# Expert arms of a perceiver's mixtures in three column tiles of 32, 32 and 64, with the small pairs' arm in front, and two weights asked for behind a context

## The chip, the cores and the metric

The kernel runs on one core of a Trainium2 chip. The metric is the device time of one execution in microseconds, the median of several runs. Beside it there is one profiled execution, whose trace holds every instruction of the engines: PE (TensorE's matmuls), PEld (TensorE's weight loads), DVE (VectorE), ACT (ScalarE), POOL (GpSimd), and SP, whose queue asks for nearly all transfers.

## What is computed

The reference is a perceiver of four levels over 2 x 64 tokens of 256 features, all in float32, with a context of 2 x 1024 rows of 192 features. Each level adds a cross attention, a second mixing layer and a feed-forward layer to `x`. The 128 tokens fill the 128 partitions. The feed-forward layers of levels 1, 2 and 3 are mixtures of 8 experts, of which each token uses its best 2:

```python
logits = xf @ gate_w
top_w, top_idx = jax.lax.top_k(logits, 2)
h = jax.nn.gelu(einsum('td,edf->tef', xf, w1) + b1)      # level 1, hidden width 1024
y = einsum('tef,efd->ted', h, w2) + b2
out = einsum('ted,te->td', y, combine)
```

Level 2 has a hidden width of 512 with a gate (`silu(g) * u`) and no biases; level 3 has a width of 1024 with a gate and biases. How many tokens an expert gets is known only when the kernel runs.

## The kernel before, in words

**Slots.** `experts` handles the 8 experts as four pairs, expert r with expert r + 4. A pair has 128 slots (columns of the gathered tokens `xg`), and a slot belongs to one of the two experts. `split[r]`, read into a register of TensorE's sequencer, says how the slots are shared: 1 means 64 and 64 ("equal"); 0 means `least` for the first expert and the rest for the second ("unequal": 32 and 96 where `least` is 32, levels 1 and 2; 0 and 128 in level 3); 2, in the levels with biases (1 and 3) and not for pair 0, means that both experts have at most 32 tokens ("small pairs").

**Tiles.** `Level.tiles_of` turns that into column tiles of the stationary operand: an equal pair gives two tiles of 64, an unequal pair of levels 1 and 2 four tiles of 32 (one for the first expert, three for the second), one of level 3 a single tile of 128. `hidden` runs, for each column half (`part`, 512 moving columns) and each of the two chunks of features, one matmul for each tile; `out_of` runs for each block of hidden features (8 in level 1, 4 in level 2) one matmul with 256 moving columns for each tile. A small pair goes through `hidden_by_halves` and `out_of_halves` instead, where each expert's 32 slots take two tiles of 32, one for each half of the hidden width. Each float32 matmul of the program shows as two MATMUL and two LDWEIGHTS rows in the trace.

**Arms.** `by_tiles` writes the arms of the branch. TensorE's sequencer compares `split[r]` and runs one arm; the others lie between in the code and are jumped over. The order of the arms in the code is: equal; unequal; small pairs. An `if` inside the `else` of the first one tells the last two apart, and where there is no arm for small pairs (a second column half), that inner `if` has no `else`.

**Order of work.** For pair r TensorE runs the hidden arm of r, gathers the tokens of r + 1, runs the output arm of r - 1, turns the products of r, and opens the sums of r + 1. After pair 3's hidden arm comes a test for tokens that found no slot, the last output arm, and the scatter. Inside the arms and between them `in_written_order` fixes the order of each engine's instructions; the SP queue is not part of that, its order is left to the scheduler.

**Weights.** `shelf.load` asks for the experts' weights in pieces of 1 MB; they lie in rotating buffers, so a transfer starts when an earlier user of its buffer is done. `l2x_w` asks for the four weights of level 2's cross attention (L132) after level 1's experts' weights. The context `crows` (`l2x_ctx`, L1976) of that attention lies in a stage pool of its own and is asked for at the beginning of that stage. Its first reader is `weigh` (L2065); `wv` is read in `project` (L2097) and `wo` in `output` (L2107).

The lines that matter below: L716 (`hidden`), L697 (`hidden_by_halves`), L690 (its biases), L773 (`out_of`), L706 (`out_of_halves`), L726 (biases), L747 (gather), L759 (turn), L787 (scatter), L409 and L411 (values of a later attention that fill a gap), L319 (matmuls that only keep TensorE busy), L800 and L808 (the comparisons).

Of the kernel before, what the change touches and what calls it, by code (L numbers as in the profile page):

```python
# [18 lines left out]
P = 128  # L19
# [39 lines left out]
def tile_perceiver(ctx: ExitStack, tc: tile.TileContext, i: dict, out: bass.AP):  # L59
# [8 lines left out]
    def stage_pool(**given):  # L68

        return tc.tile_pool(reuse_waits="tile", **given)  # L70
# [5 lines left out]
    @contextmanager  # L76
    def psum(pairs, singles):
        if psum_now["split"] != (pairs, singles):
            scope = psum_now["scope"]
            scope.close()  # L80
            psum_now.update(
                split=(pairs, singles),
                a=scope.enter_context(stage_pool(name="ps_a", bufs=pairs, space=PSUM)),
                b=scope.enter_context(stage_pool(name="ps_b", bufs=singles, space=PSUM)),
            )
        yield
# [7 lines left out]
    def stat(n=1, name="stat"):  # L94
        return small.tile([P, n], F32, tag=f"s{n}", bufs=12 if n == 1 else 4, name=name)
# [29 lines left out]
    def weight(name, index=None):  # L125
        src = i[name] if index is None else i[name][index]
        size = 4
        for n in src.shape[1:]:
            size *= n
        tag = "w2" if size <= 2048 else "w4" if size <= 4096 else "w8"  # L130
        t = wpool.tile(list(src.shape), F32, tag=tag, bufs=W_BUFS[tag], name=f"{name}_sb")
        nc.sync.dma_start(t, src)  # L132
        return t
# [148 lines left out]
    @contextmanager  # L282
    def in_written_order(behind=None):


        traced = nc.cur_bb.bb.instructions
        first = len(traced)
        last = {}
        for ins in reversed(traced):
            if ins.engine == ET.PE:  # L290
                last[ET.PE] = ins
                break
        yield last

        def put_behind(ins, other):
            tc.add_manual_dep(
                ins, other.name,
                mybir.DependencyInfo(
                    mybir.DependencyClass.NoSync, mybir.DependencyReason.DATA
                ),  # L300
                reason="in_written_order",
            )

        for ins in nc.cur_bb.bb.instructions[first:]:
            if ins.engine in (ET.PE, ET.DVE, ET.Activation, ET.Pool):
                if ins.engine in last:
                    put_behind(ins, last[ins.engine])
                elif behind and ins.engine == ET.PE:
                    for other in behind.values():
                        if other.engine != ET.Pool:  # L310
                            put_behind(ins, other)
                last[ins.engine] = ins
# [320 lines left out]
    def quarter_tile(j):  # L633
        return slice(j * 32, j * 32 + 32), j
# [4 lines left out]
    class Level:  # L639
# [24 lines left out]
        def tiles_of(self, equal):  # L664

            if equal:
                return [(slice(j * 64, j * 64 + 64), j) for j in range(2)]
            if self.least == 0:
                return [(slice(0, P), 1)]
            return [(quarter_tile(j)[0], min(j, 1)) for j in range(4)]  # L670

    def experts(level, x, shelf, pool, over_pool, fill):
        count, width, name = consts.count, level.width, level.name
# [6 lines left out]
        xg, hT, y, own, prods, split = {}, {}, {}, {}, {}, {}  # L680
# [117 lines left out]
        def by_tiles(r, behind, work, by_halves=None):  # L798

            with tc.If(split[r] == 1) as shared:  # L800
                with in_written_order(behind):
                    work(level.tiles_of(True))
            with shared.Else():
                if r == 0 or not level.halved:
                    with in_written_order(behind):
                        work(level.tiles_of(False))
                    return
                with tc.If(split[r] == 0) as other:  # L808
                    with in_written_order(behind):
                        work(level.tiles_of(False))  # L810
                if by_halves is not None:
                    with other.Else():
                        with in_written_order(behind):
                            by_halves()

        with in_written_order() as done:
            ps = bank()
# [235 lines left out]
        for h, half in enumerate(sums):  # L1053
            by_tiles(0, seen, lambda tiles: hidden(0, half, tiles))
            with in_written_order() as seen:
                if level.biases is not None:
                    add_biases(0, [half])
                gates(0, half, h)
                if half is sums[-1]:
                    ways_back()  # L1060
                    gather(1)
                    for k in range(turns):
                        if k == turns - 1:
                            fill(3)
                        turn(0, k)
                    sums = open_sums(1)
        for r in range(1, PAIRS):
            for h, half in enumerate(sums):
                by_tiles(
                    r, seen, lambda tiles: hidden(r, half, tiles),  # L1070
                    None if h else lambda: hidden_by_halves(r, half if level.gated else half[:1]),
                )
                with in_written_order() as seen:
                    gates(r, half, h)
                    if r == 1 and h == 0:
                        start_sum()
                    if h == len(sums) - 1:
                        if r + 1 < PAIRS:
                            gather(r + 1)
                        po = bank()  # L1080
            by_tiles(
                r - 1, seen, lambda tiles: out_of(r - 1, po, tiles),
                lambda: out_of_halves(r - 1, po),
# [50 lines left out]
    with psum(2, 4), stage_pool(name="l0x", bufs=1) as pool, stage_pool(  # L1134
# [5 lines left out]
        wv = pool.tile([CH + 1, 2, D], F32, name="l0x_wv")  # L1140
        m8 = pool.tile([P, NB, NK], U8, name="m8")
        wk = weight("l0x_wk")
        wlkv = weight("l0x_wlkv")
        wq = weight("l0x_wq")
# [10 lines left out]
        wo = weight("l0x_wo")  # L1155
# [349 lines left out]
    with psum(2, 4), stage_pool(name="l0a", bufs=1) as pool, in_written_order():  # L1505
        wq, wkv, wo = weight("l0a_wq"), weight("l0a_wkv"), weight("l0a_wo")
# [102 lines left out]
        r = stat(name="rstd")  # L1609
# [243 lines left out]
    with psum(3, 2), stage_pool(name="l1x", bufs=1) as pool, stage_pool(  # L1853
        name="l1x_att", bufs=3
    ) as att:
        wq, wo = weight("l1x_wq"), weight("l1x_wo")
# [90 lines left out]
    nc.sync.dma_start(l1f_bs, i["l1f_bs"])  # L1947
    for r in range(1, PAIRS):
        shelf.load(r)
    l2x_w = [weight(f"l2x_w{n}") for n in "qkvo"]  # L1950
    with psum(2, 4), stage_pool(name="l1f", bufs=1) as pool:
        last = kv3.values(1, 2)

# [16 lines left out]
    with psum(2, 4), stage_pool(name="l2x", bufs=1) as pool, stage_pool(  # L1970
        name="l2x_att", bufs=2
    ) as att, in_written_order():
        wq, wk, wv, wo = l2x_w

        crows = pool.tile([P, 16, CD + 1], F32, name="l2x_ctx")
        nc.sync.dma_start(crows[:, :, :CD], i["ctx"])  # L1976
        nc.gpsimd.memset(crows[:, :, CD:], 1.0)
        qT = pool.tile([P, 8, P], F32, name="l2x_qT")

# [578 lines left out]
    with psum(3, 2), stage_pool(name="l3x", bufs=1) as pool, stage_pool(  # L2558
        name="l3x_att", bufs=3
    ) as att:  # L2560
        wq, w1, w2, wz, wh = l3x_w
# [37 lines left out]
    with psum(2, 4), stage_pool(name="l3a", bufs=1) as pool:  # L2599
        with in_written_order():  # L2600
# [29 lines left out]
            for c in range(2):  # L2630
                for b in range(NB):
                    r = slice(b * S, (b + 1) * S)
# [188 lines left out]
```

## Time and profile before

| | before |
|---|---|
| median of 3 runs | 657.37 us (655.67 to 657.70) |
| the profiled execution, whole | 657.39 us |
| its span, first to last instruction | 655.4 us |
| mean granted TensorE clock | 0.996 |
| PE busy | 616.8 us, 94% of the span, 4722 matmul rows |
| DVE, ACT, POOL busy | 308.5, 254.8 and 49.6 us |
| HBM read | 85.98 MB, 131 GB/s over the span |

A line of the timeline gives start and duration in microseconds from the span's start, then engine, line of the kernel, operation, out<-in, the shape (rows*columns of the array for TensorE, then the moving operand) and the count; in brackets how long the engine had been idle before it and what ended that. "issue" is idle time in which the engine waited for nothing that the profile shows. A line of the groups by form gives the busy time in us and the mean of one instruction in ns behind the first bar, and the idle time ahead of the group behind the second. A matmul's duration is its latency; neighbours overlap, so the pace is read from their starts.

### The profile page before, as it was taken

The page shows a single profiled execution, that of the slowest core. Times are in us where ns is not written, and L with a number is a line of the kernel's source. Part 1 is how long each engine was busy: PE and PEld are TensorE (multiplying, and loading weights), DVE is VectorE, ACT ScalarE, POOL GpSimd, SP SyncE. Part 2 cuts the span into 40 slices and gives each one's busy share as a digit, 9 for nine tenths or more (in the row PEclk, how much of TensorE's full clock was granted, in tenths as well). Part 3 has the DMA queues.
Part 4 walks back from the last instruction along what each step waited for, and adds up shares of the span by engine and source line. Part 5 has one row for each costly group of instructions (what it writes and reads, how often), then busy time and mean ns, then how long its engine had stood idle before and what let it go on. Part 6 is the DMA issues. An engine that isn't in the chain of part 4 may idle for free. (4 is left out here: it accounts for less than half of the span.)

```text
span 655.4 us, 11703 instructions
## 1 busy us (share of the span) xinstructions
PE 616.8 (94%) x4722; PEld 451.1 (69%) x4722; DVE 308.5 (47%) x864; ACT 254.8 (39%) x503; POOL 49.6 (8%) x77
## 2 busy tenths in 40 slices
PE   7989999999999879999999988999989999999996
PEld 3547659766754448999998677999974456774444
DVE  5875452268671014555554435535435247747111
ACT  2464362378722222323223424413422149742111
POOL 3450000000100000000000040040000000000000
PEclk9999999999999989999999999999999999999999
DMA  8960025920438367000000500012047920093870
GB/s 287 407 284 1 17 74 166 316 95 2 171 117 340 111 215 283 1 1 2 1 1 1 192 1 1 1 36 94 1 136 291 384 91 1 2 380 144 349 300 11
DMA packets 19441, 87.05 MB, mean 133 GB/s; under 512 B 2080, under 2 KB 6704, under 8 KB 11088
## 3 DMA queue, kind: packets, MB, share of 16 engines
q1 hardware_dynamic: 19120, 86.09, 35.1%
q8 instruction: 49, 0.80, 0.5%
q14 instruction: 16, 0.13, 0.1%
q10 hardware_dynamic: 256, 0.03, 0.0%
HBM read 85.98 MB, written 0.13 MB: 131 GB/s over the span
## 5 line engine op out<-in xcount | busy, mean ns | idle before, releaser
L2065 PE MATMUL bank<-l2x_ctx,p 128*128 128x193 f32 x256 | 48.1, 327 | 0.0
L2065 PEld LDWEIGHTS bank<-l2x_ctx,p 128*128 128x128 f32 x256 | 40.8, 190 | 0.4
L1701 DVE CUSTOM_DVE_ANT_0 p<-two_banks,zero 128x1024 f32<-128x1024 f32 x32 | 38.6, 1217 | 5.2 <-PE two_banks L1691 5.0
L1709 ACT ACTIVATE p<-p,negmax 128x1024 f32<-128x1024 f32 x32 | 36.9, 1153 | 4.7 <-DVE negmax L1701 4.7
L2029 DVE TENSOR_REDUCE l2x_mx<-two_banks 128x128 f32<-128x1024 f32 x16 | 19.6, 1224 | 26.2 <-PE two_banks L2021 26.2
L2014 PE MATMUL two_banks<-l2x_qA,ctxA 128*128 128x128 f32 x256 | 31.9, 278 | 0.0
L2014 PEld LDWEIGHTS two_banks<-l2x_qA,ctxA 128*128 128x128 f32 x256 | 30.3, 192 | 1.1 <-issue 1.0
L765 DVE COPY m_hT<-bank 128x512 f32<-128x512 f32 x12 | 8.3, 691 | 44.7 <-PE bank L759 35.5
L319 PE MATMUL bank<-ctxA,ones 128*128 128x256 f32 x94 | 26.2, 395 | 1.0 <-DVE x_new L279 1.0
L2051 DVE TENSOR_TENSOR p<-two_banks,l2x_shift 128x512 f32<-128x512 f32 x32 | 20.6, 686 | 13.4 <-ACT l2x_shift L2046 13.4
L223 ACT ACT_TABLE_LOAD x20 | 25.7, 1283 | 0.4
L739 ACT ACTIVATE m_g<-two_banks 128x512 f32<-128x512 f32 x12 | 7.2, 597 | 47.8 <-PE two_banks L716 32.0
L740 DVE TENSOR_TENSOR m_prod<-two_banks,m_g 128x512 f32<-128x512 f32 x12 | 8.3, 690 | 35.5 <-ACT m_g L739 35.5
L2058 ACT ACTIVATE p<-p 128x512 f32<-128x512 f32 x32 | 19.6, 630 | 12.2 <-DVE p L2051 12.2
L1716 PEld LDWEIGHTS two_banks<-ident,p 128*128 128x128 f32 x128 | 13.7, 141 | 11.0 <-ACT pT L1745 9.1
L780 ACT COPY m_y<-bank 128x256 f32<-128x256 f32 x12 | 4.5, 372 | 41.6 <-PE bank L773 36.8
L319 PEld LDWEIGHTS bank<-ctxA,ones 128*128 128x128 f32 x94 | 16.1, 193 | 5.3 <-issue 2.6
L1691 PE MATMUL two_banks<-n_kT,n_qx 32*128 32x512 f32 x128 | 19.1, 640 | 0.0
L1716 PE MATMUL bank<-ident,p 128*128 128x128 f32 x128 | 18.5, 280 | 0.5
L2021 PE MATMUL two_banks<-l2x_qB,ctxB 64*128 64x128 f32 x256 | 18.6, 285 | 0.0
L1304 POOL TENSOR_SCALAR xh<-xh,cx_mv,rstd 128x192 f32<-128x192 f32 x16 | 16.8, 1062 | 15.7 <-DVE rstd L231 15.7
L2085 ACT COPY l2x_uT<-bank 96x256 f32<-96x256 f32 x16 | 5.9, 369 | 30.5 <-PE bank L2082 30.5
(608 smaller groups left out, 1336.5 us busy)
## 6 DMA issues: line engine op xcount, KB each, us to landing
l1f_w_sb<-in_l1f_w_dram SPq DMA_DIRECT2D x12, 1024.0 KB, 5.4
l3f_w_sb<-in_l3f_w_dram SPq DMA_DIRECT2D x12, 1024.0 KB, 9.3
more_w<-in_l3f_w_dram SPq DMA_DIRECT2D x12, 1024.0 KB, 9.3
l0f_w_sb<-in_l0f_w_dram SPq DMA_DIRECT2D x8, 1024.0 KB, 8.4
l2f_w_sb<-in_l2f_w_dram SPq DMA_DIRECT2D x8, 1024.0 KB, 4.8
more_w<-in_l1f_w_dram SPq DMA_DIRECT2D x4, 1024.0 KB, 6.0
more_w<-in_l2f_w_dram SPq DMA_DIRECT2D x6, 512.0 KB, 8.3
xh<-in_ctx_dram SPq DMA_DIRECT2D x8, 192.0 KB, 5.6
```

Of the source, the lines that this page charges most:

```text
L223: nc.scalar.activation(junk, behind, func, scale=0.0)
L319: nc.tensor.matmul(ps[:, :D], ones, ctxA[:, 0, 0, :D], start=True, stop=True)
L1691: nc.tensor.matmul(sc[u][:, n * 512 : (n + 1) * 512], qx[c, n][rows_, b].rearrange("p h q -> p (h q)"), kT[c, b][rows_, n, :], start=True, ...
L1701: nc.vector.tensor_tensor_reduce(p[u], sc[u], zero.to_broadcast([P, NK]), -1.0, 3.0e38, ALU.add, ALU.min, least)
L1709: nc.scalar.activation(p[u], p[u], AF.Exp, bias=sc[u], scale=-1.0, accum_out=total[u // 4][:, u % 4 : u % 4 + 1],)
L1716: nc.tensor.transpose(ps[:, kc * P : (kc + 1) * P], p[u][:, (4 * k + kc) * P : (4 * k + kc + 1) * P], ident,)
L2014: nc.tensor.matmul(sc[k][:, n, t, :], ctxA[:, b, n, t * P : (t + 1) * P], qA[:, j, b].rearrange("p h q -> p (h q)"), start=(t == 0), stop= ...
L2021: nc.tensor.matmul(sc[k][:, n, t, :], ctxB[half[n], b, t * P : (t + 1) * P], qB[half[n], j, b].rearrange("p h q -> p (h q)"), start=False, ...
L2029: nc.vector.tensor_reduce(mx[k], sc[k].rearrange("p n t q -> p q (n t)"), AX.X, ALU.max)
L2051: nc.vector.tensor_tensor(p[k][:, n], sc[k][:, n], shifts[k].unsqueeze(1).to_broadcast([P, 4, P]), ALU.add,)
L2058: nc.scalar.activation(p[k][:, n], p[k][:, n], AF.Exp)
L2065: nc.tensor.matmul(po[k][:, : CD + 1], p[k][:, kc // 4, kc % 4, :], crows[:, b * 8 + kc, :], start=(kc == 0), stop=(kc == 7),)
```

## The change

It has two parts.

1. An unequal pair of levels 1 and 2 gets three column tiles: 32 for the first expert, then 32 and 64 for the second. In `by_tiles` the inner branch of levels 1 and 3 compares with 2 instead of 0, and the small pairs' arm stands ahead of the unequal one in the code. Where there is no arm for small pairs, the inner `if` stays as it was.
2. `l2x_w` asks for `wq` and `wk` alone; `wv` and `wo` are asked for in the next stage, in the line behind the context's transfer.

```diff
-            return [(quarter_tile(j)[0], min(j, 1)) for j in range(4)]
+            return [(slice(0, 32), 0), (slice(32, 64), 1), (slice(64, P), 1)]
...
-                with tc.If(split[r] == 0) as other:
+                if by_halves is None:
+                    with tc.If(split[r] == 0):
+                        with in_written_order(behind):
+                            work(level.tiles_of(False))
+                    return
+                with tc.If(split[r] == 2) as other:
+                    with in_written_order(behind):
+                        by_halves()
+                with other.Else():
                     with in_written_order(behind):
                         work(level.tiles_of(False))
-                if by_halves is not None:
-                    with other.Else():
-                        with in_written_order(behind):
-                            by_halves()
...
-    l2x_w = [weight(f"l2x_w{n}") for n in "qkvo"]
+    l2x_w = [weight(f"l2x_w{n}") for n in "qk"]
...
-        wq, wk, wv, wo = l2x_w
+        wq, wk = l2x_w
 
         crows = pool.tile([P, 16, CD + 1], F32, name="l2x_ctx")
         nc.sync.dma_start(crows[:, :, :CD], i["ctx"])
+        wv, wo = weight("l2x_wv"), weight("l2x_wo")
         nc.gpsimd.memset(crows[:, :, CD:], 1.0)
```

In the built program TensorE loses 80 float32 matmuls of code, 56 matmul rows of them on the path that this data takes (4722 to 4666). The lists of the other engines and of the SP queue keep their instructions and their order.

## The prediction

> **What bounds the kernel now.** I read the page first, then the groups by form, then TensorE's waits, then the timeline of level 1's experts, with its weight loads. The page says which engine has no slack:
>
> ```profile
> PE 616.8 (94%) x4722; PEld 451.1 (69%) x4722; DVE 308.5 (47%) x864; ACT 254.8 (39%) x503; POOL 49.6 (8%) x77
> ...
> q8 instruction: 49, 0.80, 0.5%
> ```
>
> PE is busy 94% of the span. In the experts its rows follow each other almost without idle time (48.1 of 55.0 us in 190 to 245, 33.4 of 35.0 us in 495 to 530), so a microsecond put into an expert arm on PE is a microsecond of the kernel; nothing hides it. The second line is used further down. The groups by form give what an arm costs in each shape:
>
> ```profile
> L716 PE MATMUL two_banks<-l2f_w_sb,m_xg 128*64 128x512 f32 x32 | 7.3, 598 | 0.5 <-ACT m_xg L752 0.5
> L716 PE MATMUL two_banks<-l2f_w_sb,m_xg 128*32 128x512 f32 x64 | 7.3, 595 | 0.2 <-PE bank L759 0.2
> ```
>
> 64 rows of 32 columns take as long as 32 rows of 64: four 32-column tiles run side by side, as two of 64 do. The timeline (start, duration) gives the pace, the order of arms and the pauses:
>
> ```profile
> 199.43 1.05 PE L690 MATMUL two_banks<-l1f_bs,own 8*32 8x512 f32 x4
> 200.41 1.92 PE L697 MATMUL two_banks<-l1f_w_sb,m_xg 128*32 128x512 f32 x16
> ...
> 214.07 0.63 PE L706 MATMUL bank<-more_w,m_hT 128*32 128x256 f32 x4
> 216.28 1.92 PE L706 MATMUL bank<-more_w,m_hT 128*32 128x256 f32 x28 [1.58 <-issue]
> ...
> 220.84 3.64 PE L716 MATMUL two_banks<-l1f_w_sb,m_xg 128*32 128x512 f32 x32
> 224.41 3.67 PE L773 MATMUL bank<-l1f_w_sb,m_hT 128*64 128x256 f32 x32
> ...
> 230.20 1.03 PE L409 MATMUL two_banks<-l3x_wv_sb,ctxA 128*128 128x256 f32 x4
> 231.16 0.70 PE L411 MATMUL two_banks<-l3x_wv_sb,ctxB 64*128 64x256 f32 x4
> 231.79 2.56 PE L773 MATMUL bank<-l1f_w_sb,m_hT 128*32 128x256 f32 x41
> 236.83 2.62 PE L773 MATMUL bank<-l1f_w_sb,m_hT 128*32 128x256 f32 x23 [2.48 <-issue]
> ```
>
> The 32-column rows of L716 and L773 say which arms run unequal: in level 1 pair 3 (hidden at 220.84, output at 231.79), in level 2 pairs 1 and 2 (hidden at 502.46 and 509.74, output at 513.96 and 520.62). Pair 1 of level 1 runs by halves (L697, L706). Level 3 has no 32-column tiles outside its halves, and its one unequal pair is a single 128-column tile, untouched.
>
> **Prices.** The loads of the same arm show the steps of four rows:
>
> ```profile
> 221.30 0.13 PEld L716 LDWEIGHTS two_banks<-l1f_w_sb,m_xg 128*32 128x32 f32 x4 [0.30 <-issue]
> 221.72 0.13 PEld L716 LDWEIGHTS two_banks<-l1f_w_sb,m_xg 128*32 128x32 f32 x4 [0.30 <-issue]
> ```
>
> A step of 512 moving columns takes 0.43 us; one of 256 takes 0.216 (32 rows of 64 columns in 3.67 us). Each float32 matmul of the program is two rows in the trace, so four tiles take two steps now: 0.86 us in the hidden layer, 0.43 in the output.
>
> A change of tile shape is the price that decides. I compared the starts of neighbouring matmul rows over the whole trace. Neighbours of one shape follow with 2 to 5 ns beyond the stream. Of 248 neighbours of different shape (rows or columns rounded up to 32, 64 or 128), 228 wait 90 to 97 ns beyond the full stream of the former, 20 wait longer, none less. L409 to L411 shows it above: 4 x 0.216 + 0.095 = 0.96 us. L690 to L697 shows that disjoint columns do not escape: the biases use column quarters 1 and 3, the first tile behind them quarter 0, and it still starts 0.98 us later, two streams of 0.43 plus 0.1. The first step in a new shape is also slower, by about 0.025 us for 32 columns and 0.05 for 64 (0.266 against 0.216 at 224.41).
>
> **The three tiles.** No row here mixes 32 and 64 columns inside an arm, so I bound it. From below: three tiles side by side, 0 us. From above: each on its own, six streams in place of two. I take the row nearest to it, the drain at each change of shape: two 32-column tiles together (two steps), a change, the 64-column tile alone (two steps), a change.
> - Hidden: 4 x 0.43 + 2 x 0.095 + 0.075 = 1.985 us against 0.86, so +1.125 for each of the 4 groups (2 column halves x 2 chunks) of an arm; three arms, 12 groups: +13.5.
> - Output: 4 x 0.216 + 0.19 + 0.075 = 1.13 against 0.43, so +0.70; 8 groups in level 1 and 4 in each of two pairs of level 2, 16 groups: +11.2.
> - The last change of each of the six arms is there already: -0.6.
>
> Together +24.1 us. The 56 rows and 56 loads that fall away save nothing by themselves, since the streams and not the issue pace the steps. Without the slower first steps it would be +22.0.
>
> [...]
>
> **Arms' order.** One branch is exchanged for another, so the branches cost nothing; what moves is where the code lies. The two "issue" pauses (1.58 and 2.48 us) wait on nothing that the profile shows. Counting the program's PE instructions from the first pause to the second, skipped arms included, gives 768, three times 256; q8 moved 49 packets in 0.80 MB, 16.4 KB each. So I take one packet to be a block of 256 instructions, and a pause to be a block that arrives late, behind the weight transfers of 194 to 214 us and 224 to 238 us. Before the first pause only 8 matmul rows lie in the last block, before the second 51 under the 1.75 MB asked for at 228.1 and 228.5. Behind the second the clock is granted at half for 3.4 us, which makes 23 rows last 2.6 us and costs about 1.4 more. Pauses now: 1.6 + 2.5 + 1.4 = 5.5 us. With 80 matmuls' code gone and the arms exchanged, the same count puts 46 rows between the blocks around pair 1's output, so that pause goes. In pair 3 one block border falls at the jump into the output arm, 18 rows after the one before: a pause of 0 to 1.5 us; the next is covered by an arm that has become long. I take 4.5 saved, bounds 5.5 saved and, if a border falls worse, 4 lost.
>
> **The two weights.** The line that asks for l2x_wv and l2x_wo now stands behind the context's transfer, but in the built program the queue's order is unchanged: wq, wk, wv, wo, context, with the same waits. That half does nothing: 0 us. Were it to work, little would ask for it: the context is asked for at 241.16, lands 8.2 us later, and is first used at 259.5; wv is first used at 274.8.
>
> **Sum.** The profiled execution took 657.39 us, a span of 655.4 and 2.0 around it, level with the median of 657.37. +24.1 - 4.5 = +19.6, so 677.0.
>
> **Rivals.**
> - Side by side (0.11): the array takes 32, 32 and 64 columns at once. The matmul cost is 0, the pauses fall by about 3 (the last block is then less covered), 654 us: faster. It decides if the 64-column row starts within 10 ns of the 32-column rows. Against it: no change of shape in this trace was free.
> - Side by side and the pauses only move (0.03): 657, no change.
> - Nothing overlaps, not even the two small tiles (0.04): six streams a group where the drain case has four, 12 x 0.86 + 16 x 0.43 = 17.2 more: 694. Against it: 64-column tiles pair today in the same order of rows.
>
> **How the numbers follow.** The drain has 0.82. Its low end: only one of the two changes in a group is paid, 28 x 0.145 = 4.1 less, with 5.5 of pauses saved: +14.5, 672. Its high end: 24.1 with 4 us of new pauses: +28, 686 rounded up. The range 672 to 686 leaves out the rivals, 0.18. A measurement of this kernel tells about 0.3%, 2 us, from no change. Slower 0.86 (drain and serial), faster 0.11, same 0.03.
>
> **What would show it.** Right: L716's 32-column rows halved to 16 in level 1 and 32 in level 2, each of the three hidden arms 7.5 to 8.1 us instead of 3.64, level 1's output arm near 9 instead of 3.7 without its pause, and steps where the 64-column row starts a full stream behind. The pause at L706 gone, the one at L773 under 1.5 us. Transfers of wv and wo still ahead of the context. Wrong: hidden arms still at 3.6 us, or a pause of over 4 us in pair 3.

## The result and the profile after

The changed kernel takes 674.56 us (median of 4 runs, 674.22 to 675.00) against 656.93 us for the kernel before beside it: 1.0268 times as long, 95% interval 1.0252 to 1.0285. It is slower by 17.6 us. The forecast was 677.0 in a range of 672 to 686. The profiled execution took 674.41 us with a span of 672.6, that is 17.2 more than the span before. The half clock that the trace of before shows behind the second pause (0.50 for 3.4 us) is, going by the mean clock, not in every execution of that kernel: of 17 later ones, the four with a mean granted clock of 0.999 or more took 654.8 to 655.2 us, the eleven with 0.997 or less 656.2 to 658.3.

The page after, the lines that answer to those of before:

```profile
PE 637.8 (95%) x4666; PEld 453.2 (67%) x4666; DVE 308.4 (46%) x864; ACT 254.8 (38%) x503; POOL 50.0 (7%) x77
...
q8 instruction: 48, 0.79, 0.5%
```

TensorE runs 56 matmul rows fewer and is busy 21 us longer. The other engines do the same work in nearly the same time (DVE 308.4 us against 308.5, ACT 254.8 in both, POOL 50.0 against 49.6).

The groups by form of the changed kernel, level 2's hidden arms:

```profile
L716 PE MATMUL two_banks<-l2f_w_sb,m_xg 128*64 128x512 f32 x48 | 15.9, 605 | 0.5 <-ACT m_xg L752 0.5
L716 PE MATMUL two_banks<-l2f_w_sb,m_xg 128*32 128x512 f32 x32 | 8.4, 604 | 0.1
```

The 32-column rows of level 2 halved in number (64 to 32) and their busy time rose from 7.3 to 8.4 us. The 64-column rows rose from 32 to 48, their time from 7.3 to 15.9 us: the 16 new ones have nothing beside them (the two rows of each such matmul start 0.48 us apart, as at 518.40 and 518.88, with no other row between them).

The weight loads inside level 1's mixed hidden arm (start, duration, in brackets the idle time of the load unit before):

```profile
219.38 0.19 PEld L716 LDWEIGHTS two_banks<-l1f_w_sb,m_xg 128*64 128x64 f32 x2 [0.84 <-issue]
220.38 0.14 PEld L716 LDWEIGHTS two_banks<-l1f_w_sb,m_xg 128*32 128x32 f32 x4 [0.81 <-issue]
221.37 0.19 PEld L716 LDWEIGHTS two_banks<-l1f_w_sb,m_xg 128*64 128x64 f32 x2 [0.84 <-issue]
222.37 0.14 PEld L716 LDWEIGHTS two_banks<-l1f_w_sb,m_xg 128*32 128x32 f32 x4 [0.81 <-issue]
```

The widths alternate, and each waits for the other: from 220.38 to 222.37 one group of three tiles takes 1.99 us, where four tiles of 32 columns took two steps of 0.43. The loads, too, of the next width start only when the former width's rows have streamed through: the one at 219.38 stands 0.52 us behind the start of the last 32-column row (218.86), a stream of 0.43 and 0.1 more. In the whole trace 51 pairs of neighbouring matmul rows change between 32 and 64 columns, and the second of each starts 94 to 97 ns behind the full stream of the first.

The timeline of TensorE, the arms named in the prediction, in level 1 and, from 517.43 on, one hidden and one output arm of level 2:

```profile
213.82 1.93 PE L706 MATMUL bank<-more_w,m_hT 128*32 128x256 f32 x32
...
218.40 7.58 PE L716 MATMUL two_banks<-l1f_w_sb,m_xg 128*32 128x512 f32 x23
225.34 0.65 PE L773 MATMUL bank<-l1f_w_sb,m_hT 128*64 128x256 f32 x2
225.82 0.59 PE L716 MATMUL two_banks<-l1f_w_sb,m_xg 128*64 128x512 f32 x1
225.83 4.04 PE L773 MATMUL bank<-l1f_w_sb,m_hT 128*64 128x256 f32 x30
...
234.10 9.12 PE L773 MATMUL bank<-l1f_w_sb,m_hT 128*32 128x256 f32 x48 [0.59 <-PE two_banks L411]
243.16 0.70 PE L319 MATMUL bank<-ctxA,ones 128*128 128x256 f32 x2
...
517.43 8.01 PE L716 MATMUL two_banks<-l2f_w_sb,m_xg 128*32 128x512 f32 x24
525.37 0.71 PE L747 MATMUL bank<-m_pick,xl 128*128 128x128 f32 x4
526.01 4.60 PE L773 MATMUL bank<-more_w,m_hT 128*32 128x256 f32 x24
530.54 0.66 PE L759 MATMUL bank<-ident,m_prod 128*128 128x128 f32 x4
```

(A merged line bears the form of its first row.) L706 runs through without its pause, the mixed output arm lasts 9.06 us from its first row to the next work, and the pause ahead of it is 0.59 us.

The SP queue of the changed kernel asks in the order of before:

```profile
229.48 0.33 SPq L132 DMA_DIRECT2D l2x_wv_sb<-in_l2x_wv_dram  x1
229.90 0.38 SPq L132 DMA_DIRECT2D l2x_wo_sb<-in_l2x_wo_dram  x1
244.57 0.61 SPq L1980 DMA_DIRECT2D l2x_ctx<-in_ctx_dram  x1
```

### The profile page after: what moved, and what is told of

Its sections match the earlier page's. It is cut to its first block, busy times and chain, and to the rows that moved or that the text cites. A ratio compares the mean times of both kernels' runs of the same rounds, so it can differ in the third digit from the quotient of the medians.

```text
span 672.6 us, 11593 instructions
## 1 busy us (share of the span) xinstructions
PE 637.8 (95%) x4666; PEld 453.2 (67%) x4666; DVE 308.4 (46%) x864; ACT 254.8 (38%) x503; POOL 50.0 (7%) x77
## 5 line engine op out<-in xcount | busy, mean ns | idle before, releaser
L2034 DVE TENSOR_REDUCE l2x_mx<-two_banks 128x128 f32<-128x1024 f32 x16 | 19.6, 1224 | 26.2 <-PE two_banks L2026 26.2
L319 PE MATMUL bank<-ctxA,ones 128*128 128x256 f32 x94 | 25.6, 389 | 1.0 <-DVE x_new L279 1.0
L2063 ACT ACTIVATE p<-p 128x512 f32<-128x512 f32 x32 | 19.6, 630 | 12.2 <-DVE p L2056 12.2
L716 PE MATMUL two_banks<-l2f_w_sb,m_xg 128*64 128x512 f32 (+1 forms) x80 | 23.3, 604 | 0.6 <-ACT m_xg L752 0.5
L319 PEld LDWEIGHTS bank<-ctxA,ones 128*128 128x128 f32 x94 | 16.0, 190 | 4.8 <-issue 2.2
```

The lines of the kernel that those rows point to most:

```text
L319: nc.tensor.matmul(ps[:, :D], ones, ctxA[:, 0, 0, :D], start=True, stop=True)
L716: nc.tensor.matmul(part[s], xg[r][:, c, s], shelf.at[r, j, n](c, f), start=((none_yet or r == 0) and c == 0), stop=(none_yet and c == 1), ...
L2034: nc.vector.tensor_reduce(mx[k], sc[k].rearrange("p n t q -> p q (n t)"), AX.X, ALU.max)
L2063: nc.scalar.activation(p[k][:, n], p[k][:, n], AF.Exp)
```

## Experiments

Six kernels separate the three edits, the two theories of the three tiles (a drain at each change of width, which is the prediction's word for the wait of 94 to 97 ns behind the full stream; or something in the exchanged arms) and the two theories of the pauses (code that comes late behind weight transfers, or the jumps themselves). Times that are compared were taken side by side on one chip; the kernel before stood at 656.43 us beside the first four of them and at 656.53 beside the last two.

**The three tiles alone** (`e1_tiles_only`). The kernel before with one line changed:

```diff
-            return [(quarter_tile(j)[0], min(j, 1)) for j in range(4)]
+            return [(slice(0, 32), 0), (slice(32, 64), 1), (slice(64, P), 1)]
```

> The kernel before with the three tiles alone; arms in the old order, weights asked for as before. Theory (a change of column width drains TensorE): as slow as the changed kernel, 674.5 us within 1; each of the three mixed hidden arms 7.9 us, level 1's mixed output arm 9.1. The code borders fall as in the changed kernel (46 rows before the one behind pair 1's output, 18 before the one at pair 3's output), so both long pauses are gone here too. Rival (the exchanged arms cost the time): 657 or less, hidden arms 3.6 us.

Measured: 675.02 us, ratio 1.0281 (1.0261 to 1.0301), as slow as the whole change. The hidden arms are as long as in the changed kernel, level 2's 8.01 us, level 1's output arm 9.06, and of the pauses 0.52 us ahead of that arm is left:

```profile
517.87 8.01 PE L716 MATMUL two_banks<-l2f_w_sb,m_xg 128*32 128x512 f32 x24
```

```profile
234.52 9.12 PE L773 MATMUL bank<-l1f_w_sb,m_hT 128*32 128x256 f32 x48 [0.52 <-PE two_banks L411]
243.58 0.70 PE L319 MATMUL bank<-ctxA,ones 128*128 128x256 f32 x2
```

The whole loss is the tiles', and in this code the exchanged arms bring nothing on top.

**The arms exchanged alone** (`e2_order_only`), four tiles of 32:

```diff
-                with tc.If(split[r] == 0) as other:
+                with tc.If(split[r] == 2) as other:
                     with in_written_order(behind):
-                        work(level.tiles_of(False))
+                        by_halves()
...
```

> The kernel before with the arms exchanged alone, four tiles of 32. Theory (a pause is a block of 256 instructions that comes late): the border behind pair 1's output moves from 8 rows to 36 rows after the one before it, so the 1.6 us pause at L706 goes or shrinks below 0.4; the border in pair 3's output arm moves from 41 rows into the arm to 7 rows into it, while the block comes no earlier, so the pause at L773 grows from 2.5 us to 3.5 to 4.5 and sits after about 7 rows. Together 655.5 to 658. Rival (a pause is the price of a jump to a far arm): pair 3's arm, now further back, pauses before its first row, and the pause does not sit at 7 rows.

Measured: 657.54 us, ratio 1.0017 (1.0004 to 1.0031). The timeline of level 1, pair 3's output arm:

```profile
229.42 0.63 PE L773 MATMUL bank<-l1f_w_sb,m_hT 128*32 128x256 f32 x7
234.27 5.66 PE L773 MATMUL bank<-l1f_w_sb,m_hT 128*32 128x256 f32 x57 [4.21 <-issue]
```

The pause sits behind the 7th row, where counting 256 instructions from the pauses of before had put the border, and is 4.2 us long. The rival's pause, ahead of the arm's first row, is not there: that row follows L411 after 0.63 us (228.79, 229.42), as it did before (231.16, 231.79). The granted clock is at half for 6.8 us (its mean over 229 to 245 us is 0.79, 0.89 before), of which the first 2.2 lie inside the pause (3.4 us before, all behind it); that fits the 57 rows behind the pause, which take 5.58 us here and 3.33 at full clock in the fifth kernel. L706 has no pause any more; 0.6 us is left in front of the next L759, more than the 0.4 that I had written. So the exchange takes away one pause, lengthens the other, and on balance costs 1.1 us.

**The two weights really behind the context** (`e4_weights_behind`). The kernel before, with the edit of the change to `l2x_w` and an order that the scheduler must keep:

```diff
         nc.sync.dma_start(crows[:, :, :CD], i["ctx"])
+        asked = nc.cur_bb.bb.instructions[-1]
+        wv, wo = weight("l2x_wv"), weight("l2x_wo")
+        for ins in nc.cur_bb.bb.instructions[-2:]:
+            tc.add_manual_dep(
+                ins, asked.name,
+                mybir.DependencyInfo(
+                    mybir.DependencyClass.NoSync, mybir.DependencyReason.DATA
+                ),
+                reason="behind the context",
+            )
```

> The kernel before, with level 2's wv and wo really held behind the context's transfer by an order between the three. Theory (the late block of code waits behind the 1.75 MB of wv and wo): the pause of 2.5 us in pair 3's output arm falls below 0.6 and the half clock behind it goes, so 3.5 to 4.5 us faster, about 652.8; the pause of 1.6 us at pair 1 stays. wv lands before 274. Rival (the pause comes from the place of the code and the jumps alone): the pause stays at 2.5 us and the time at 657.

Measured: 653.36 us, ratio 0.9945 (0.9928 to 0.9963), 3.1 us faster, where 3.5 to 4.5 had been expected. Between the two traces the stretch from pair 1's L726 to the first L409 behind pair 3's output arm shrinks by 4.2 us (33.5 to 29.3); that the medians lie closer fits the executions of the kernel before that lack the half clock. Its waits of TensorE, and the same output arm in its timeline:

```profile
PE bank L706 <- issue: 1.7, 1, 1.7
```

```profile
232.54 3.66 PE L773 MATMUL bank<-l1f_w_sb,m_hT 128*32 128x256 f32 x64
236.13 0.70 PE L319 MATMUL bank<-ctxA,ones 128*128 128x256 f32 x2
```

TensorE's code is laid out as before, with the same border 41 rows into the arm, and the 64 rows run through in 3.59 us at full clock (1.00 over 229 to 245 us); the pause at pair 1, ahead of which those two transfers had not been asked for, stays (1.71 us, 1.58 before). So the second pause came from wv and wo. In the trace of before q8's packet ahead of the border starts at 234.2 us, long after the two transfers were asked for at 228.1 and 228.5; here it starts at 232.0, before the arm's first row. That this packet is the block of code behind the border is inferred: the count of 256 names the row, and the rows resume 1.4 to 1.6 us behind the end of such a packet wherever there is a pause (the numbers stand with the fifth kernel, `e6_order_behind`).

**The three tiles grouped by width** (`e5_grouped`). The changed kernel, each unequal arm going first over all 32-column tiles, then over the 64-column one:

```diff
-            for part, n, f, _ in half:
-                for c in range(2):
-                    for s, j in tiles:
+            for part, n, f, c, s, j in [
+                (part, n, f, c, s, j) for kind in (small_ones, wide) for part, n, f, _ in half
+                for c in range(2) for s, j in kind
+            ]:
...
```

> The changed kernel, with the three tiles' matmuls ordered by width inside each unequal arm: first all of the 32-column tiles, then all of the 64-column tile. Theory (a drain at each change, and no overlap across widths): a hidden arm takes 16 steps of 0.43 and one change, 7.05 us instead of 7.94; level 1's output arm 7.1 instead of 9.1, level 2's 3.6 instead of 4.5; in all 6.4 less than the changed kernel, 668.2 us. Rival A (the price is the change alone, widths otherwise overlap): arms near 3.8 us, 652. Rival B (three tiles cost what they cost in any order): 674.5.

Measured: 668.70 us, ratio 1.0185 (1.0164 to 1.0205); 6.3 us less than the three tiles alone beside it; 6.4 less than the changed kernel, 668.2 us, had been expected. Level 2's hidden arm and output arm:

```profile
503.34 7.20 PE L719 MATMUL two_banks<-l2f_w_sb,m_xg 128*32 128x512 f32 x24
510.47 0.71 PE L750 MATMUL bank<-m_pick,xl 128*128 128x128 f32 x4
...
521.97 3.79 PE L779 MATMUL bank<-more_w,m_hT 128*32 128x256 f32 x24
525.69 0.65 PE L762 MATMUL bank<-ident,m_prod 128*128 128x128 f32 x4
```

7.13 and 3.72 us from start to start: one change of width in place of seven, and still twice the steps of four 32-column tiles. So of the loss about a quarter (6.3 us) is the changes themselves and the rest is that rows of different width did not run side by side here. Rival A (3.8 us arms) and rival B (no gain) both fall. For rival A this order is the weaker test, since it puts the 64-column rows behind all of the 32-column ones in the program; the stronger one is the changed kernel, where the widths alternate and no 64-column row started beside a 32-column one.

**Both kinds of pause together** (`e6_order_behind`): the exchanged arms with wv and wo held behind the context.

> The kernel before with the arms exchanged (four tiles of 32) and wv and wo held behind the context. Theory (late blocks of code): the pause at pair 1 is gone as in the exchange alone; in pair 3's output arm the border lies 7 rows in, and its block waits behind wq and wk only, so the pause there is 0.5 to 1.5 us instead of 4.2, with little or no half clock behind it: 652 to 654 us. Rival (arms' order as such costs time): slower than 654.5, or a pause before the arm's first row.

Measured: 652.37 us, ratio 0.9938 (0.9921 to 0.9956). The pause is behind the 7th row again, now 1.15 us long, with the clock full behind it (1.00 over 190 to 245 us):

```profile
229.45 0.63 PE L773 MATMUL bank<-l1f_w_sb,m_hT 128*32 128x256 f32 x7
231.23 3.40 PE L773 MATMUL bank<-l1f_w_sb,m_hT 128*32 128x256 f32 x57 [1.15 <-issue]
```

The pauses and q8's packets keep step. In this kernel the packet ahead of the pause's end runs from 228.8 to 229.7 us, with the arms exchanged alone from 231.6 to 232.8, in the kernel before from 234.2 to 235.4; the rows resume 1.5, 1.5 and 1.4 us after its end. For the pause at pair 1 the same time is 1.4 us before and 1.6 with the weights really behind the context.

**The exchange for pairs 1 and 2 alone** (`e8_order_early_behind`), with wv and wo behind the context: the new order of arms only where `r < PAIRS - 1`.

> As the last one, but the arms are exchanged for pairs 1 and 2 only; pair 3 keeps the old order, so that the border lies 41 rows into its output arm. Theory: no long pause is left in level 1, since the border at pair 1 comes 36 rows after the one before it and the one at pair 3 has its block in time: 651.4 us, 2.0 less than with wv and wo held back alone, and faster than the kernel before and the changed kernel. Rival (only the transfers matter): 653.4, with a pause at pair 1.

Measured: 651.85 us, ratio 0.9928 (0.9912 to 0.9943); 651.4 had been expected. Pair 3's output arm runs through:

```profile
229.58 3.66 PE L773 MATMUL bank<-l1f_w_sb,m_hT 128*32 128x256 f32 x64
```

Level 1's arms have no pause left that waits for nothing the profile shows, but for 0.40 us ahead of L759. This kernel is the fastest of all, 4.7 us under the kernel before beside it and about 3.4% under the changed one. That it is better than the last kernel is not settled: the two medians lie 0.5 us apart.

## Why the prediction was right

**The three tiles: right in cause and size.** Forecast +24.1 us. A mixed group of the hidden layer was put at 1.985 us and took 1.99; level 1's output arm at 9.0 and took 9.06. Measured against the arms of before: level 1's hidden arm and the output arm behind it +4.2 (from 220.84 to 228.02 then, 218.40 to 229.79 now), its own output arm +5.5 (9.06 against the 3.59 that it takes without a pause), level 2's hidden arms +4.4 each (7.94 against 3.57), its output arms +2.7 each (4.53 against 1.86): 23.7 in all before rounding. The row that decided was L690 to L697, where disjoint column quarters did not start together. It was weaker than I took it to be: the rows of the array change there (8 to 128), the column width stays at 32. No row of before held 32 and 64 columns in one arm, so that the price would carry over was a choice; the first experiment shows that it does. My count of neighbours was also too clean: four changes, from and to the 8-column rows of L968 (196.42 and 603.97), follow with 2 to 3 ns, so "none less" and "no change of shape was free" are wrong for them. They bear on no arm here. What the traces show is the wait, about 0.095 us at each change; what the array does in it, they do not show.

**The pauses: right in place, too small.** I took 4.5 us saved, with 5.5 as the most. From start to start the pause at pair 1 had cost 2.2 us (4.06 from L706's first row to L759, against 1.87 now), the one at pair 3 with the half clock in its arm 4.0 (7.59 against 3.59), and the half clock on the two rows of L319 behind it another 0.4: 6.6. What the change left is 0.6, in the place and the bounds forecast; the profile puts its end down to L411 and not to issue, and no run tells what it waits for. 6.0 saved in place of 4.5, and outside my bound of 5.5: this is the mis-sized term of the sum. I took the idle times that the waits list, 1.6 and 2.5, which begin at the modelled end of the last row; from start to start the pauses cost 2.2 and 2.9. The half clock cost 1.5, near the 1.4 that I had. The remaining 0.3 us lies ahead of level 1's experts: their first row starts at 190.26 instead of 190.51, and no run shows a reason for it.

**The sum.** 23.7 - 6.0 - 0.3 = 17.4; the spans differ by 17.2. The forecast of 19.6 was 2 us too high, and most of that is the pauses.

**The two weights: nothing, as forecast,** and for the reason given: the queue kept its order. What I did not see is that the edit would have been worth something. I judged it by its own readers, who have time to spare, and not by what stands behind those transfers: by the inference from the fourth kernel, `e4_weights_behind`, the code block of pair 3. The kernel with the two really behind the context shows 3.1 us for it in the code of before.

**The rivals.** Side by side fell with the first arm; nothing overlaps at all fell too, since the two 32-column tiles still start 7 ns apart in the arms.

## What to carry to other kernels

Count the steps of an arm by width: in the changed kernel no row of 64 columns ran beside one of 32 (94 to 97 ns behind the full stream at each of 51 changes), so four equal tiles beat three unequal ones (3.6 us against 7.9 for a hidden arm), and 56 matmul rows fewer bought nothing where the streams set the pace. A pause that waits for nothing in an instruction stream with branches is worth a count of instructions and a look at the transfers asked for just before: here holding back two weights that nobody needed yet (3.1 us) gave more than any change to the arms. After an edit to the order of transfers, look at the queue's order in the result, not at the line where the request is written.

## What had not been expected of the hardware

- Across two arms of the changed kernel, tiles of one width did run side by side: the next output arm's first 64-column rows (L773 at 225.34) started 0.48 us before the last 64-column row of the mixed hidden arm (L716 at 225.82), the second row of a matmul that stands ahead of them in the program.
- Around two of the pauses the granted clock was at half: with start gaps of 2.9 us (before) and 4.6 us (arms exchanged) for 3.4 and 6.8 us, from 0.2 us behind the first gap and from 2.2 us ahead of the end of the second; with the 2.0 us gap at pair 1 it stayed full (1.00 over 214 to 218 us). In the kernel before it seems not to do so in every execution: 3.4 us at half would take 0.003 off the mean clock, and four of 17 had a mean of 0.999 or more.
- The pause was longer with more weights already asked for: with the border at the same 7th row, the pause was 4.21 us behind wv and wo and 1.15 us without them.
